# Four graph layers on 32 pairs of graphs: the pairs under way start 14 steps apart instead of 7

## The chip, the core and the metric

The kernel runs on one core of a Trainium2 chip. The metric is the time of one execution on the device in microseconds (us). The engines of the core work side by side, each through its own queue in order: TensorE (PE in the profile; its weight loads are PEld), VectorE (DVE), ScalarE (ACT), GpSimd (POOL), and SyncE (SP), which issues the transfers. TensorE writes into PSUM, which VectorE and ScalarE read; the rest lies in SBUF.

## What is computed

64 graphs of 256 nodes with 256 features go through four layers. Each normalizes x, cuts it off at 0, applies a graph layer and adds the result to x. All of it is float32.

```python
# layer 0: 8 heads of 32, softmax over the neighbours (adj > 0), output projection
h = relu(layernorm(x)); x = x + mha(h, adj, Wq, Wk, Wv) @ Wo + bo
# layer 1: e = leaky(f1[i] + f2[j]), masked by adj, softmax over axis 1, elu of the sum
h = relu(layernorm(x)); x = x + elu(softmax(where(adj > 0, e, -9e15), axis=1) @ (h @ W))
# layer 2: three rounds of a gated unit on the sums over the neighbours
h = relu(layernorm(x))
for i in range(3): h = gru(A.T @ (h @ weight[i]), h)
x = x + h
# layer 3: 4 heads of 64, additive attention, softmax over the neighbours (adj == 1)
h = relu(layernorm(x)); x = x + gat(h, adj, W, b, a)
```

## The kernel before, in words

Two graphs, a **pair**, go through all four layers together, so there are 32 pairs. A pair's x and adj are loaded as one tile each (io pool, 4 buffers), and x stays in SBUF until layer 3 has stored it. Each layer is a generator: a `yield` ends a **step**, and a pair takes 44 steps.

- Layer 0, steps 1 to 13: mask mb0 and norm (L268, L226 to L234); transposes psn and hT (L241, L243); q, k, v (L278, L250); then for each of 4 row blocks a `scores` step (pss L300, s = min(scaled scores, mask) L307, row maxima mx L260, eight exponentials with sums L262) and an `attend` step (16 transposes pst L327, copies to pT by VectorE L334 and ScalarE L332, psc L341 with pT as weights and 32-wide moving operands, ctxs L348), the scores one block ahead; then transposes psct and the projection pso (L250).
- Layer 1, steps 14 to 18: mask (L379 to L391), norm, one softmax over 256 columns (L409 to L421), product psh (L427), elu and sum (L435 to L438).
- Layer 2, steps 19 to 33: mask am and norm, then three times four steps: psgm and its copy m (L250, L451); psa and its copy aT (L457, L465); the gates r, hn and n (L475, L491 to L507); gate z and the new state hg (L491, L494, L512 to L514). The products of the gates are 512 wide. At the end hg is transposed back (psx L520) and added to x (L521).
- Layer 3, steps 34 to 44: mask mb3 (L526, L527), norm, f and sd (psf L536, L537; pssd L548, copies by ScalarE L549), then 4 blocks of `scores` (L554 to L561, L260, four exponentials L262) and `attend` (8 transposes pst L572, copy eT by ScalarE L574, pso L580, o L588, sum on GpSimd L594); the last one issues the store.

The main loop at the end sets the order. Up to three pairs are under way, and in each turn of the loop each of them takes one step, the oldest first. A new pair starts when the youngest has taken at least `LEAD` steps and fewer than three are under way. With 44 steps and a lead of 7, the first three start at turns 0, 7 and 14; the fourth starts when the first has ended, and so the pattern of 0, 7 and 14 repeats each 44 turns, a **round** of three pairs. Three pairs of a round are called its first, second and third below. The last round has two pairs.

The framework gives each instruction to its engine's queue nearly in this order, but may put a later instruction that it takes to be ready ahead of an earlier one; on the chip each queue is then in order. Buffers come from pools, by tag: `w4` (token tiles, 17 buffers), `w8` (scores and their transposes, 4), `hT` (4), `f3` (1, L530), `mask` (2), and PSUM tiles of two banks (4). A tile waits until a buffer of its tag is released.

```python
            ps = bank2(f"psc_{p}_{t}")
            for i in range(H0):
                h = 4 * (i % 2) + i // 2
                for c in range(2):
                    mm(ps[:, 0, h * D0 : (h + 1) * D0], pT[:, i, c, :],
                       v[:, 2 * g + c, h * D0 : (h + 1) * D0], start=c == 0, stop=c == 1)
```

Of the kernel before, what the change touches and what calls it, by code (L numbers as in the profile page):

```python
# [9 lines left out]
FP = mybir.dt.float32  # L10
# [5 lines left out]
P = 128  # L16
# [8 lines left out]
def tile_adj_preln_d4(  # L25
# [18 lines left out]
    a3: bass.AP,  # L44
    out: bass.AP,
):
    """Four pre-norm graph layers on B graphs of N nodes.

    Two graphs go through all layers together. "Token" tiles are [node in chunk, t, feature] with
    t = 2 * graph + chunk; "T" tiles are [feature in chunk, feature chunk, 2 * N nodes].  # L50
    """
    nc = tc.nc
    B, N, D = x.shape
    NL = ggw.shape[0]
    H0, H3 = 8, a3.shape[0]
    D0, C3 = D // H0, D // H3
    assert N == 2 * P and D == 2 * P and B % 2 == 0 and H0 == 8 and H3 == 4
    T = 4  # token tiles in a pair
    N2 = 2 * N
    SCALE = 1.0 / math.sqrt(D0)  # L60

# [2 lines left out]
    psum = ctx.enter_context(tc.tile_pool(name="psum", bufs=4, space=bass.MemoryType.PSUM))  # L64

    def bank2(name):
        """Two PSUM banks."""
        return psum.tile([P, 2, 512], FP, tag="ps", name=name)

    def flat(ap):  # L70
# [10 lines left out]

    loaded = {0: loads(0)}

# [1 line left out]
    ident = const.tile([P, P], FP, name="ident")  # L85
    make_identity(nc, ident)
    mhalf = const.tile([P, T], FP, name="mhalf")
# [39 lines left out]
    with tc.tile_pool(name="prep", bufs=1) as prep:  # L127

        def transposed(dst, src, rows):
            """dst[:, k, :] = rows k of the transpose of src [P, rows / P, D]."""  # L130
            n = rows // P
            for k in range(2):
                for o in range(0, n, 4):
                    m = min(4, n - o)
                    ps = bank2(f"tw_{k}_{o}")
                    for i in range(m):
                        nc.tensor.transpose(
                            ps[:, 0, i * P : (i + 1) * P],
                            src[:, o + i, k * P : (k + 1) * P],
                            ident,  # L140
                        )
                    nc.vector.tensor_copy(dst[:, k, o * P : (o + m) * P], ps[:, 0, 0 : m * P])

        for w, wT, nm in ((w_ih, wihT, "wih_sb"), (w_hh, whhT, "whh_sb")):
            t = prep.tile([P, 6, D], FP, tag="wg", bufs=2, name=nm)
            nc.sync.dma_start(t, w.rearrange("(k p) d -> p k d", p=P))
            transposed(wT, t, 3 * D)
        # r and z are taken as (1 + tanh(v / 2)) / 2.
        nc.vector.tensor_add(brz, bih_sb[:, 0:4], bhh_sb[:, 0:4])
        nc.vector.tensor_scalar_mul(brz, brz, 0.5)  # L150

        # Layer 1: f1 = h (W a_1), f2 = h (W a_2).
        w1T = prep.tile([P, 2, D], FP, name="w1T")
        transposed(w1T, w1a, D)
        a1_sb = prep.tile([P, 2, 2], FP, name="a1_sb")
        nc.sync.dma_start(a1_sb.rearrange("p w k -> p (w k)"), a1.rearrange("(c p) e -> p (c e)", p=P))
        for f in range(2):
            ps = bank2(f"wa_{f}")
            for k in range(2):
                mm(ps[:, 0, 0:2], w1T[:, k, f * P : (f + 1) * P], a1_sb[:, :, k], start=k == 0, stop=k == 1)  # L160
            wa = prep.tile([P, 2], FP, tag="wa", bufs=2, name=f"wa_sb_{f}")
            nc.vector.tensor_copy(wa, ps[:, 0, 0:2])
            nc.vector.tensor_copy(wa1_bc[:, f, :], wa[:, 0:1].to_broadcast([P, P]))
            nc.vector.tensor_copy(w1a[:, f, D : D + 1], wa[:, 1:2])

        # Layer 3: s_src = h (W^T a_src) + b a_src, s_dst likewise; a's rows on a block diagonal.
        w3_sb = prep.tile([P, 2, D], FP, name="w3_sb")
        nc.sync.dma_start(w3_sb, w3.rearrange("(k p) o -> p k o", p=P))
        transposed(w3a, w3_sb, D)
        blk = prep.tile([P, 2, 2, H3], FP, name="blk")  # L170
        nc.vector.memset(blk, 0.0)
        for h in range(H3):
            r0 = (h * C3) % P
            for w in range(2):
                nc.sync.dma_start(
                    blk[r0 : r0 + C3, h * C3 // P, w, h : h + 1],
                    a3[h : h + 1, w * C3 : (w + 1) * C3].rearrange("o c -> c o"),
                )
        for f in range(2):
            ps = bank2(f"w3s_{f}")  # L180
            for k in range(2):
                mm(
                    ps[:, 0, 0 : 2 * H3],
                    w3_sb[:, k, f * P : (f + 1) * P],
                    blk[:, k].rearrange("p w h -> p (w h)"),
                    start=k == 0,
                    stop=k == 1,
                )
            nc.vector.tensor_copy(w3a[:, f, D : D + H3], ps[:, 0, 0:H3])
            ws = prep.tile([P, H3], FP, tag="ws", bufs=2, name=f"ws_{f}")  # L190
            nc.vector.tensor_copy(ws, ps[:, 0, H3 : 2 * H3])
            nc.vector.tensor_copy(wdst_bc[:, f], ws.unsqueeze(2).to_broadcast([P, H3, P]))
        b3_sb = prep.tile([P, 2], FP, name="b3_sb")
        nc.sync.dma_start(b3_sb, b3.rearrange("(k p) -> p k", p=P))
        b3_w = prep.tile([P, 2, P], FP, name="b3_w")
        nc.vector.tensor_copy(b3_w, b3_sb.unsqueeze(2).to_broadcast([P, 2, P]))
        blk_s = prep.tile([P, 2, H3], FP, name="blk_s")
        nc.vector.tensor_add(blk_s, blk[:, :, 0, :], blk[:, :, 1, :])
        ps = bank2("b3s")
        for k in range(2):  # L200
            mm(ps[:, 0, 0:H3], b3_w[:, k, :], blk_s[:, k, :], start=k == 0, stop=k == 1)
        nc.vector.tensor_copy(b3a_bc[:, D : D + H3], ps[:, 0, 0:H3])

# [1 line left out]
    work = ctx.enter_context(tc.tile_pool(name="work", bufs=2))  # L205
    small = ctx.enter_context(tc.tile_pool(name="small", bufs=4))

    def w4(name):
        """A token tile."""
        return work.tile([P, T, D], FP, tag="w4", bufs=17, name=name)  # L210

    def w4T(name):
        return w4(name).rearrange("p (a b) d -> p a (b d)", a=2)
# [2 lines left out]
        return work.tile([P, H0, N], FP, tag="w8", bufs=4, name=name)  # L216

    def mask(name):
        return work.tile([P, T, N], FP, tag="mask", bufs=2, name=name)

    def norm_relu_T(xt, nm):
        """T tile of relu(layernorm(xt))."""
        st = small.tile([P, T, 6], FP, tag="st", name=f"st_{nm}")
        mv = small.tile([P, T, 2], FP, tag="mv", name=f"mv_{nm}")
        for t in range(T):
            nc.vector.bn_stats(st[:, t, :], xt[:, t, :])  # L226
        for t in range(T):
            nc.vector.bn_aggr(mv[:, t, :], st[:, t, :])  # L228
        rs = small.tile([P, T], FP, tag="rs", name=f"rs_{nm}")
        nc.gpsimd.tensor_scalar_add(rs, mv[:, :, 1], EPS)  # L230
        nc.gpsimd.tensor_tensor(rs, rs, mhalf, ALU.pow)
        xn = w4(f"xn_{nm}")
        for t in range(T):
            nc.vector.tensor_scalar(  # L234
                xn[:, t, :], xt[:, t, :], mv[:, t, 0:1], rs[:, t : t + 1], ALU.subtract, ALU.mult
            )
        yield
        ps = bank2(f"psn_{nm}")
        for k in range(2):
            for t in range(T):  # L240
                nc.tensor.transpose(ps[:, k, t * P : (t + 1) * P], xn[:, t, k * P : (k + 1) * P], ident)  # L241
        hT = work.tile([P, 2, N2], FP, tag="hT", bufs=4, name=f"hT_{nm}")
        nc.scalar.activation(hT, ps, AF.Relu)  # L243
        return hT

    def token_mm(rhs, hT, ps4):
        """ps4[t] = h rhs, node chunk by node chunk."""
        for t in range(T):
            for k in range(2):
                mm(ps4[t], hT[:, k, t * P : (t + 1) * P], rhs[:, k, :], start=k == 0, stop=k == 1)  # L250
# [4 lines left out]
        return v, [v[:, t, :] for t in range(T)]  # L255

    def exp_rows(e, n, zs, nm):
        """e[:, i] = exp(e[:, i] - max) in place for i < n, and their sums in zs."""
        mx = small.tile([P, n], FP, tag=f"mx{n}", name=f"mx_{nm}")
        nc.vector.tensor_reduce(mx, e, AX.X, ALU.max, negate=True)  # L260
        for i in range(n):
            nc.scalar.activation(  # L262
                e[:, i, :], e[:, i, :], AF.Exp, bias=mx[:, i : i + 1], accum_out=zs[:, i : i + 1]
            )

    def layer0(xt, at, p):
# [7 lines left out]
        for w, nm in ((wq_sb, "q"), (wk_sb, "k")):  # L274
# [4 lines left out]
            t = w4T(f"{nm}T_{p}")  # L279
# [5 lines left out]
        v = w4(f"v_{p}")  # L285
# [2 lines left out]

        ctxs = w4(f"ctxs_{p}")

        # Head h = 4 * cc + hh lies on partitions 32 * hh of feature chunk cc; rows are (hh, cc).
        def scores(t):
            g = t // 2
            s = w8(f"s_{p}_{t}")
# [146 lines left out]
    def layer2(xt, at, p):  # L441
# [4 lines left out]
        for l in range(NL):  # L446
# [60 lines left out]
                nc.scalar.activation(hn[:, o, :], hn[:, o, :], AF.Tanh, bias=bih_sb[:, 4 + o : 5 + o])  # L507
            yield
            z = sigmoid(2, "z")
            # (1 - z) n + z h = n + z (h - n)  # L510
            hnew = work.tile([P, 2, N2], FP, tag="hT", bufs=4, name=f"hg_{nm}")
            nc.gpsimd.tensor_sub(hnew, hT, hn)  # L512
            nc.vector.tensor_mul(hnew, hnew, z)
# [98 lines left out]
        for layer in (layer0, layer1, layer2, layer3):  # L612
            yield from layer(xt, at, p)

    # Pairs start LEAD steps apart, so that one's matrix products fill another's softmax and norms.
    LEAD, UNDER_WAY = 7, 3
    active, p = [], 0
    while active or p < B // 2:
        if p < B // 2 and (not active or (len(active) < UNDER_WAY and active[-1][1] >= LEAD)):
# [39 lines left out]
```

## Time and profile before

| | |
|---|---|
| median of three timed runs | 6370.5 us (6350.5 to 6374.0) |
| the profiled execution, first to last instruction | 6365.3 us |
| mean granted TensorE clock in it | 0.890 of full speed |
| TensorE matmul busy | 5787.0 us (91%), 24500 records |
| TensorE weight load busy | 3967.9 us (62%) |
| VectorE busy | 3090.6 us (49%) |
| ScalarE busy | 2004.0 us (31%) |
| GpSimd busy | 777.0 us (12%) |
| transfers | 58.4 MB, 9 GB/s over the span |

The page gives the span of the profiled execution, 6365.3 us; the timed runs have no profile, and their median is 5.2 us above it. A float32 product stands in the trace as two records, a transpose as one. A group of instructions is named by its line, its engine and its tiles (out<-in); buffer and pair numbers are left out, so that psn is the transposed norm of any layer, and `pso` is the projection of layer 0 at L250 and the output of layer 3 at L580. In a list of waits each line gives who waited for whom, the total, the number of times and the longest one. A granted clock of 1.00 is full speed.

### The profile page before, as it was taken

The numbers are of one execution on the slowest core, as the hardware profiler recorded it, in microseconds if no ns is written. First come the engines' busy times: TensorE is split into PE (matmuls) and PEld (weight loads), VectorE is DVE, ScalarE is ACT, GpSimd is POOL, SyncE is SP. The second block draws the span as 40 slices with busy tenths as digits, with TensorE's granted clock in tenths as the row PEclk, the third lists the DMA queues.
The fourth block names the chain that finished last, engine by engine and source line by source line (L and its number), as shares of the span: only waits on it lengthen the run. The fifth ranks groups of instructions, "written<-read, shape, count | busy, mean of one in ns | idle before, by whom it ended". The sixth has DMA issues, their size and how long they took to land.

```text
span 6365.3 us, 60565 instructions
## 1 busy us (share of the span) xinstructions
PE 5787.0 (91%) x24500; PEld 3967.9 (62%) x24500; DVE 3090.6 (49%) x4479; ACT 2004.0 (31%) x4737; POOL 777.0 (12%) x582
## 2 busy tenths in 40 slices
PE   7998899889989988998899889889988998999887
PEld 6655765666566556655765665576557656665755
DVE  4435534554454445445544553554455345534534
ACT  2323322332233233223322332242233223322422
POOL 1011101100110111011001101110110011001011
PEclk7899799889978997898899889978987998899798
DMA  1000000000000000000000000000000000000000
GB/s 53 1 4 19 9 1 7 17 7 1 14 17 1 4 14 14 1 4 20 7 1 14 17 1 4 14 14 1 4 20 7 1 7 17 7 1 10 7 0 7
DMA packets 58279, 58.40 MB, mean 9 GB/s; under 512 B 4752, under 2 KB 58000, under 8 KB 58000
## 3 DMA queue, kind: packets, MB, share of 16 engines
q1 hardware_dynamic: 58000, 54.54, 2.6%
q8 instruction: 192, 3.15, 0.2%
q14 instruction: 87, 0.71, 0.0%
HBM read 37.76 MB, written 16.78 MB: 9 GB/s over the span
## 4 chain that ended last, share of the span: by engine, by line
PE 78%; DVE 13%; ACT 8%; issue 1%; DMA 0%; POOL 0%; SPq 0%; ACTq 0%; POOLq 0%; DVEq 0%
PE psr L475 10%; PE psz L475 10%; PE psc L341 9%; PE psin L475 5%; PE pshn L475 5%; PE psa L457 5%; PE pso L580 5%; PE psgm L250 4%; PE pssd L548 3%; PE pss L300 3%; DVE mx L260 3%; PE psq L278 2%; ACT s L262 2%; PE pso L250 2%; PE psf L536 2%; ACT eT L574 2%
## 5 line engine op out<-in xcount | busy, mean ns | idle before, releaser
L341 PE MATMUL psc<-v,pT 128*128 128x32 f32 x4096 | 621.6, 316 | 146.1 <-DVE pT L334 143.6
L341 PEld LDWEIGHTS psc<-v,pT 128*128 128x128 f32 x4096 | 612.1, 237 | 198.7 <-DVE pT L334 92.6
L262 ACT ACTIVATE s<-s,mx 128x256 f32<-128x256 f32 x1024 | 506.8, 499 | 304.5 <-DVE mx L260 166.0
L262 ACT ACTIVATE e<-e,mx 128x256 f32<-128x256 f32 x640 | 318.0, 500 | 630.6 <-DVE mx L260 630.5
L580 PE MATMUL pso<-f,eT 128*128 128x64 f32 x2048 | 323.1, 324 | 193.6 <-ACT eT L574 193.5
L580 PEld LDWEIGHTS pso<-f,eT 128*128 128x128 f32 x2048 | 302.8, 234 | 228.9 <-ACT eT L574 228.9
L307 DVE SCALAR_TENSOR_TENSOR s<-pss,mb 128x1024 f32<-128x1024 f32 x256 | 306.8, 1219 | 176.4 <-PE pss L300 176.4
L457 PE MATMUL psa<-am,m 128*128 128x256 f32 x1536 | 369.5, 396 | 2.3 <-ACT m L451 2.2
L475 PE MATMUL psz<-aT,wihT 128*128 128x512 f32 x768 | 363.6, 596 | 0.0
L475 PE MATMUL psr<-aT,wihT 128*128 128x512 f32 x768 | 363.3, 593 | 0.0
L475 PE MATMUL psin<-aT,wihT 128*128 128x512 f32 x768 | 345.2, 592 | 0.0
L457 PEld LDWEIGHTS psa<-am,m 128*128 128x128 f32 x1536 | 298.8, 199 | 47.6 <-ACT m L451 7.2
L327 PE MATMUL pst<-ident,s 128*128 128x128 f32 x2048 | 297.7, 307 | 18.7 <-DVE pT L334 14.5
L494 DVE TENSOR_SCALAR z<-z 128x1024 f32<-128x1024 f32 x96 | 66.6, 693 | 493.9 <-ACT z L491 493.9
L327 PEld LDWEIGHTS pst<-ident,s 128*128 128x128 f32 x2048 | 278.2, 163 | 32.8 <-DVE pT L334 17.1
L260 DVE TENSOR_REDUCE mx<-s 128x8 f32<-128x2048 f32 x128 | 292.0, 2281 | 1.2
L243 ACT ACTIVATE hT<-psn 128x1024 f32<-128x1024 f32 x128 | 130.9, 1022 | 488.8 <-PE psn L241 488.7
L348 DVE TENSOR_TENSOR ctxs<-psc,rz 128x256 f32<-128x256 f32 x128 | 54.4, 425 | 459.7 <-PE psc L341 459.7
L230 POOL TENSOR_SCALAR rs<-mv 128x4 f32<-128x4 f32 x128 | 33.7, 263 | 1973.1 <-DVE mv L228 1730.7
L475 PEld LDWEIGHTS psz<-aT,wihT 128*128 128x128 f32 x768 | 148.6, 194 | 191.0 <-issue 191.0
L250 PE MATMUL psgm<-gg_sb,hg 128*128 128x256 f32 x1024 | 254.4, 405 | 14.4 <-DVE hg L514 14.4
L594 POOL TENSOR_TENSOR x<-o,x 128x256 f32<-128x256 f32 x128 | 118.9, 929 | 1177.9 <-DVE o L588 1164.4
(140 smaller groups left out, 10040.8 us busy)
## 6 DMA issues: line engine op xcount, KB each, us to landing
x<-in_x_dram SPq DMA_DIRECT2D x32, 512.0 KB, 3.4
adj<-in_adj_dram SPq DMA_DIRECT2D x32, 512.0 KB, 3.3
out_dram<-x SPq DMA_DIRECT2D x32, 512.0 KB, 2.9
gg_sb<-in_L_gnn_weight_dram SPq DMA_DIRECT2D x3, 256.0 KB, 6.3
wih_sb<-in_L_gnn_w_ih_dram SPq DMA_DIRECT2D x1, 768.0 KB, 6.4
whh_sb<-in_L_gnn_w_hh_dram SPq DMA_DIRECT2D x1, 768.0 KB, 7.2
wq_sb<-in_L_gnn_Wq_dram SPq DMA_DIRECT2D x1, 256.0 KB, 5.4
wk_sb<-in_L_gnn_Wk_dram SPq DMA_DIRECT2D x1, 256.0 KB, 5.6
```

Of the source, the lines that this page charges most:

```text
L243: nc.scalar.activation(hT, ps, AF.Relu)
L250: mm(ps4[t], hT[:, k, t * P : (t + 1) * P], rhs[:, k, :], start=k == 0, stop=k == 1)
L260: nc.vector.tensor_reduce(mx, e, AX.X, ALU.max, negate=True)
L262: nc.scalar.activation(e[:, i, :], e[:, i, :], AF.Exp, bias=mx[:, i : i + 1], accum_out=zs[:, i : i + 1])
L300: mm(ps[:, j, cc * N : (cc + 1) * N], qT[r : r + D0, cc, t * P : (t + 1) * P], kT[r : r + D0, cc, g * N : (g + 1) * N], start=True, stop=True,
L307: nc.vector.scalar_tensor_tensor(s[:, 4 * half : 4 * half + 4, :], ps.rearrange("p a (b d) -> p (a b) d", d=N), SCALE, mb0[:, t : t + 1, : ...
L327: nc.tensor.transpose(psr[:, 2 * i + c, :], s[:, 4 * half + i, c * P : (c + 1) * P], ident)
L341: mm(ps[:, 0, h * D0 : (h + 1) * D0], pT[:, i, c, :], v[:, 2 * g + c, h * D0 : (h + 1) * D0], start=c == 0, stop=c == 1,)
L457: mm(psa[:, o, g * N : (g + 1) * N], m[:, 2 * g + c, o * P : (o + 1) * P], am[:, 2 * g + c, :], start=c == 0, stop=c == 1,)
L475: mm(ps[:, o, :], w[:, k, c0 : c0 + P], src[:, k, :], start=n == 0, stop=n == 2 * len(terms) - 1,)
L548: mm(ps[:, j, :], wdst_bc[:, k, 2 * half + j, :], hT[:, k, :], start=k == 0, stop=k == 1)
L580: mm(pso[:, 0, h * C3 : (h + 1) * C3], eT[:, 2 * h + c, :], f[:, 2 * g + c, h * C3 : (h + 1) * C3], start=c == 0, stop=c == 1,)
```

## The change

The lead becomes 14 steps, about a third of the 44. The three pairs of a round then start at turns 0, 14 and 28, and this pattern repeats. `mask` gets a third buffer, and `w4` 16 buffers instead of 17; a buffer of either takes 4 KB of each partition. Nothing else of the program changes but comments.

```diff
     def w4(name):
-        return work.tile([P, T, D], FP, tag="w4", bufs=17, name=name)
+        return work.tile([P, T, D], FP, tag="w4", bufs=16, name=name)
...
     def mask(name):
-        return work.tile([P, T, N], FP, tag="mask", bufs=2, name=name)
+        return work.tile([P, T, N], FP, tag="mask", bufs=3, name=name)
...
-    LEAD, UNDER_WAY = 7, 3
+    LEAD, UNDER_WAY = 14, 3
     active, p = [], 0
     while active or p < B // 2:
         if p < B // 2 and (not active or (len(active) < UNDER_WAY and active[-1][1] >= LEAD)):
```

## The prediction

> **What bounds the kernel now.** I read first the page's busy shares and slices, then stretches of one round of three pairs, then TensorE's waits, then the order of time around them.
>
> ```profile
> PE 5787.0 (91%) x24500; PEld 3967.9 (62%) x24500; DVE 3090.6 (49%) x4479; ACT 2004.0 (31%) x4737; POOL 777.0 (12%) x582
> PE   7998899889989988998899889889988998999887
> PEclk7899799889978997898899889978987998899798
> ```
> TensorE is the busiest by far, but its digits and its clock dip together, about ten times: once in each round of three pairs. A round is 587.5 us: TensorE starts psq of pair 3 at 594.3 us and of pair 30 at 5882.0, and (5882.0 - 594.3) / 9 = 587.5. One round, cut by how many pairs are in layer 2 (none, one, two, one):
>
> ```profile
> 2356.00:2573.00 217.00, 186.16 (x997) 146.82 (x995) 121.50 (x163) 84.20 (x241) 25.13 (x20) 0.79 0.04 13
> 2573.00:2677.00 104.00, 99.81 (x422) 68.67 (x422) 44.32 (x71) 28.27 (x63) 8.92 (x8) 0.91 0.00 1
> 2677.00:2851.00 174.00, 169.98 (x554) 99.59 (x553) 69.40 (x97) 45.78 (x76) 17.79 (x11) 0.99 0.01 3
> 2851.00:2948.00 97.00, 83.73 (x325) 52.95 (x323) 53.81 (x88) 29.23 (x64) 20.63 (x15) 0.94 0.05 17
> ```
> The columns are length, busy PE, PEld, DVE, ACT, POOL, then the granted clock. With no pair in layer 2 TensorE idles 31 of 217 us and its clock is 0.79; with two it idles 4 of 174 at 0.99. The clock is worth as much as the idle time:
>
> ```profile
> 2372.23 2.00 PE L580 MATMUL pso<-f,eT 128*128 128x64 f32 x16 [1.16 <-ACT eT L574]
> ...
> 2407.52 3.68 PE L580 MATMUL pso<-f,eT 128*128 128x64 f32 x16 [1.10 <-ACT eT L574]
> ```
> The same 16 matmuls take 2.00 us and 3.68 us: the trace's clock record knows only full and half speed. From start to start at full speed a 512-wide matmul record takes 0.43 us, a 256-wide one 0.217, psc 0.113, pso of layer 3 0.115, a transpose 0.111, pss 0.09. Times the counts of the groups: 4608 x 0.43 (L475) + 5632 x 0.217 + 1152 x 0.43 (L278, L396, L548) + 4096 x 0.113 + 2048 x 0.115 + 4864 x 0.111 + 2048 x 0.09 = 5120 us, 160 a pair, 480 a round. The span is then 5120 work + 578 idle (6365.3 - 5787.0) + 667 lost mostly to half clock. In rounds 2 to 10 (5289 us, 4846 busy): **480 work + 49 idle + 58 half clock = 587**. The change can touch only the last two. Who ends the idle time:
>
> ```profile
> PE pso L580 <- ACT eT L574: 193.5, 127, 5.9
> PE psc L341 <- DVE pT L334: 143.6, 97, 4.7
> PE psx L520 <- DVE hg L514: 88.9, 22, 6.8
> PE psn L241 <- DVE xn L234: 44.6, 12, 5.2
> ```
> The columns are total us, times, longest. The first two are built into the steps: transposes, a copy, and the matmuls that read the copy stand in a row on TensorE.
>
> **The change, part by part.** No instruction is added or removed. (1) The mask buffer more and the w4 buffer less: the trace shows no wait for either. A pair holds one mask at a time, so three pairs need three. For w4 I bound the loss by the f3 buffer's waits (L530 has one; VectorE waits for it at L537 21 times, 208 us in all, and TensorE's pso then waits 5.9 us instead of 1.2): from nothing to 32 x 5 = 160 us. I take nothing, since the order below holds no trace of a shortage. (2) f3's conflict ends: with 14 steps between, layer 3 of one pair is over before the next writes f3. TensorE gets back 10 x 4.5 us = 4.5 a round. (3) The head and tail: 44 steps a pair, so 491 steps become 498. (4) The order. The order of instructions of the two built programs (without times) shows what TensorE finds between a producer's last matmul and the consumer that waits for it. I call the sum of full-speed matmul time between them the cover, and match it with the waits that the same link had before.
>
> - pT to psc: always 0.9 us of cover in both. Before 145.9 us for 128 groups; 0.9 a group without the long ones. Ten a round: **9 us**.
> - eT to pso: no cover 127 times before, 118 after, 1.2 us each when nothing else is late. Eleven a round: **13 us**.
> - hg to psx or psgm: before, cover 0 gave waits of 6.8 us, 3.5 gave 1.3, over 5 none. After there is one psgm without cover (about 5), one psx with 0.9 (6), three with 2.7 to 4.2 (1.3 each): **15 us**, against 10.
> - Out of layer 1. psh's output goes through L435 to L438, the norm and xn before psn can start, and this chain is 9 us of VectorE, ScalarE and GpSimd work with nothing between. Before, the cover was 9 us or more in every round, and only one pair in three waited:
>
> ```profile
> 3128.30 1.23 DVE L435 TENSOR_SCALAR ex<-psh 128x1024 f32<-128x1024 f32 x1 [2.23 <-PE psh L427]
> ...
> 3141.51 2.27 DVE L260 TENSOR_REDUCE mx<-s 128x8 f32<-128x2048 f32 x1
> ...
> 3145.53 1.38 DVE L234 TENSOR_SCALAR xn<-x,mv,rs 128x256 f32<-128x256 f32 x4 [0.35 <-POOL rs L231]
> ```
> Another pair's L307 and mx stand between on VectorE's queue. After, the cover is 13.3, 3.8 and 1.8 us for a round's first, second and third pair, because the next pair now enters layer 0 just there. I walk the queues by hand: 1.15 us for a 1024-wide VectorE operation in a row, 2.2 for mx, 1.7 for stats and aggregates, 1.5 for GpSimd's rs. *Second pair*, psh's end at 0: L435 from 1.0, then L307, L437, L307, L438 to 6.8, mx to 9.0, L521 to 10.2, norm to 11.9, rs to 13.4, psn at 14.0; TensorE has work until 3.8: **10.2 us**. Next on VectorE are L307, mx and the other pair's norm, so pT ends at 21.1 where pst was done at 17: **4.2 us** at psc. *Third pair*: psh waits 2.1 for wh, psn 6.3: **8.4 us**.
> - *First pair*: psn is covered, but the psc that follows is not. The next pair's pT stands behind layer 3's e, which waits for the sd copies that ScalarE makes after eight exponentials: mx 8.3, exponentials 13.9, sd 15.9; then five operations of 1.15, mx 2.2 and mx 1.1 to 25.2, pT to 26.4. pst is done at 16: **10.3 us**.
>
> Idle in a round: 9 + 13 + 15 + 10.2 + 4.2 + 8.4 + 10.3 = **70 us**, against 49.
>
> Half clock. By the clock record, a whole psc group beside a layer 2 (the third pair before) cost 2.3 to 3.3 us, without layer 2 up to 7.2; groups that the order cuts in two by a wide matmul cost nothing; layer 3's pso 0.9 on the mean; psx's 6.8 us wait about 2.5. After: 7 whole psc x 2.9 = 20, two psc that run into a pso at 5 = 10, 8 other pso x 0.9 = 7, three long waits x 2.5 = 7.5, and the two psc behind a 10 us wait 4 more each = 8: **52 us**, against 58. Layer 2 beside every softmax ends each half-clock spell sooner, but no longer gives TensorE a stretch without any.
>
> A round: 480 + 70 + 52 = **602 us**, nine 5418. *Head*: 352 us of work up to psq of pair 3 (before 453). Setup 28; the first 68 us of work are pair 0 alone, with waits such as the trace's first ones and norms without cover, 30 idle and 20 half clock: 118; the rest 284 x 602/480 = 356: 502. *Tail*, from psq of pair 30: 448 us of work. 317 x 602/480 = 398; 107 of the last layer 2 beside one layer 3, with 24 of waits and 8 of clock: 139; then the last layer 3 alone, about 68 from its last psz (before 79 from 6286.5 to the end, with a rest of pair 30 in it): 605. Sum 5418 + 502 + 605 = 6525, against the profiled 6365.3. The median of the runs is 5.2 above that span; so **6530 us**, 2.5% more.
>
> [...] With TensorE as in the stretch of two layers 2 (170 of 174 us busy) a round would be near 500 and the kernel near 5500; the walks above speak against it. [...]
>
> **Rivals.** *A, evenly fed TensorE wins* (faster): the walks fail, say because a late TensorE lets VectorE clear its queue. Idle 40 (49 less f3's 4.5 and psn's 4.2), half clock 9 x 2.9 + 8 + 3 = 37: a round 557, head 475, tail 575, in all 6065. For it: the clock of 0.91 to 0.99 beside layer 2. Against it: before, one layer 2 at a time (2573 to 2677, 2851 to 2948) had 18 idle us in 201, no better than the mean. It decides if the four long waits come out under some 4 us each. *B, half of it*: the long waits at half length, idle 60, half clock 50: a round 590, head 495, tail 597, in all about 6405. *C, worse*: w4 waits or more half clock, 625 a round: about 6755. *D, it doesn't do what it says*: excluded by the order, which has one pair in layer 2 at nearly every step.
>
> **How the numbers follow.** Forecast (6450 to 6650) 0.55, B (6320 to 6450) 0.25, A 0.13, C 0.07. The range leaves out most of A and C: 6290 to 6680. Faster by over 0.5% (about what a measurement of this kernel can tell from no change) takes A and a little of B: 0.16; within 0.5% 0.14; slower 0.70.
>
> **What would show it.** Slices without the ten dips in PE and PEclk; L537's wait for pso gone; TensorE's wait of psn for xn at some 15 us a round (44.6 in all before, over 140 after), of psc for pT over 200 in all; mean clock about 0.90 still. I am wrong if psn's and psc's waits stay where they were, or if the mean clock rises above 0.93.

## The result and the profile after

The changed kernel takes 6593.9 us (median of four runs, 6588.1 to 6597.0) against 6366.7 (6350.5 to 6374.0) for the kernel before in the same runs: a ratio of 1.0368, 95% interval 1.0348 to 1.0387. The forecast was 6530, and slower. The profiled execution spans 6589.3 us at a granted clock of 0.881 (before 6365.3 at 0.890).

The page of the kernel after, its first part and two rows of its slices:

```profile
PE 5828.3 (88%) x24500; PEld 3965.9 (60%) x24500; DVE 3105.2 (47%) x4479; ACT 2009.4 (30%) x4737; POOL 790.0 (12%) x582
...
PE   7898889889888988898898898888998899898887
...
PEclk7898899888889888898889898988888899889887
```
The ten dips of before are gone, as foretold, but so are many of the nines (12 of 40 slices of PE, against 19). TensorE is busy 41 us longer (5828.3 against 5787.0) with the same instructions, and idle for 761 us against 578.

One round, cut where TensorE starts psq of the second, third and next first pair; columns as in the prediction (length, busy PE, PEld, DVE, ACT, POOL, granted clock, DMA):

```profile
2330.40:2523.20 192.80, 175.72 (x747) 118.02 (x747) 85.37 (x125) 58.64 (x137) 24.92 (x18) 0.89 0.03 9
2523.20:2719.10 195.90, 174.45 (x741) 119.83 (x740) 91.27 (x127) 61.84 (x147) 19.68 (x15) 0.88 0.02 6
2719.10:2941.40 222.30, 194.99 (x808) 131.70 (x807) 113.45 (x168) 67.73 (x160) 29.34 (x22) 0.88 0.03 10
```
Each third idles 17 to 27 us at 0.88 or 0.89. Before, stretches from 0.79 to 0.99 stood side by side. The load is even, and evenly poor. TensorE's waits in the kernel after:

```profile
PE psn L241 <- DVE xn L234: 167.7, 38, 8.1
PE psc L341 <- DVE pT L334: 161.8, 127, 6.9
PE pso L580 <- ACT eT L574: 150.6, 118, 3.1
PE psgm L250 <- DVE hg L514: 109.2, 44, 4.7
PE psx L520 <- DVE hg L514: 59.9, 21, 5.3
```
psn's wait for xn went from 44.6 to 167.7 us and psgm's for hg from 14.4 to 109.2; pso's fell from 193.5 to 150.6 and psx's from 88.9 to 59.9. VectorE's wait for pso at L537, 208 us before, is no longer in its list.

Where the time is lost is best seen in **rounds**. I take the stretch from psq of pair 3 to psq of pair 30, nine rounds; idle is its length less busy PE; the rest is what is left over the 480 us of full-speed work. Half speed is the time per round in which the trace's clock record stands at half. TensorE is idle in some of it: 9.8 us a round before, 20.8 after. By the durations of the records I estimate that some 5 or 6 us of the rest, in both kernels, are not half speed.

| kernel | round, us | idle | rest | half speed |
|---|---|---|---|---|
| before | 587.5 | 49.2 | 58.3 | 121.7 |
| after | 608.8 | 65.1 | 63.7 | 139.2 |

So of 21.3 us more in a round 15.9 are idle time and 5.4 are clock; nine rounds make 191 of the 224 us by which the span grew. The rest is in the head, 504.3 us, and the tail, 606.2 (before 594.3 and 483.3).

Which products paid for the clock is seen in the groups of matmuls. First the kernel before (busy, mean ns of one | idle time just before them):

```profile
L457 PE MATMUL psa<-am,m 128*128 128x256 f32 x1536 | 369.5, 396 | 2.3 <-ACT m L451 2.2
...
L300 PE MATMUL pss<-kT,qT 32*128 32x256 f32 x2048 | 259.7, 565 | 0.4
...
L250 PE MATMUL psgm<-gg_sb,hg 128*128 128x256 f32 x1024 | 254.4, 405 | 14.4 <-DVE hg L514 14.4
```
and the same three after:

```profile
L457 PE MATMUL psa<-am,m 128*128 128x256 f32 x1536 | 454.7, 462 | 3.6 <-ACT m L451 3.6
...
L250 PE MATMUL psgm<-gg_sb,hg 128*128 128x256 f32 x1024 | 368.8, 538 | 109.2 <-DVE hg L514 109.2
...
L300 PE MATMUL pss<-kT,qT 32*128 32x256 f32 x2048 | 165.7, 407 | 23.8 <-DVE s L307 23.8
```
psc and pso of layer 3 cost the same in both (619 against 622, 321 against 323). But before, pss often stood in half-speed spells behind psc: 1254 of its 2048 records began in such a spell, and in groups of 16 that ran wholly at half speed one took 131 ns on the mean, against a median of 72 in those at full speed. After, 56 begin there. psa and psgm stand there now (189 records before, 1138 after), and such a record takes 427 ns instead of 216. They pay 200 us more (85.2 and 114.4 by the lines), pss 94 less. All other groups together cost some 64 less (pst 50 and psq 29 of it, with some others up), which leaves the 41 us.

### The profile page after: what moved, and what is told of

Read it like the earlier page. It is cut to its first block, busy times and chain, and to the rows that moved or that the text cites. A ratio compares the mean times of both kernels' runs of the same rounds, so it can differ in the third digit from the quotient of the medians.

```text
span 6589.3 us, 60281 instructions
## 1 busy us (share of the span) xinstructions
PE 5828.3 (88%) x24500; PEld 3965.9 (60%) x24500; DVE 3105.2 (47%) x4479; ACT 2009.4 (30%) x4737; POOL 790.0 (12%) x582
## 4 chain that ended last, share of the span: by engine, by line
PE 72%; DVE 18%; ACT 7%; issue 1%; POOL 1%; DMA 0%; SPq 0%; DVEq 0%; ACTq 0%; POOLq 0%
PE psr L475 9%; PE psc L341 9%; PE psz L475 8%; PE psgm L250 8%; PE psa L457 7%; PE pshn L475 4%; PE pso L580 4%; PE psin L475 3%; DVE mx L260 3%; PE pssd L548 2%; DVE s L307 2%; DVE pT L334 2%; PE psq L278 2%; PE psn L241 2%; ACT s L262 2%; PE pso L250 2%
## 5 line engine op out<-in xcount | busy, mean ns | idle before, releaser
L341 PE MATMUL psc<-v,pT 128*128 128x32 f32 x4096 | 619.0, 315 | 174.6 <-DVE pT L334 161.8
L262 ACT ACTIVATE e<-e,mx 128x256 f32<-128x256 f32 x640 | 316.9, 496 | 556.1 <-DVE mx L260 556.1
L250 PE MATMUL psgm<-gg_sb,hg 128*128 128x256 f32 x1024 | 368.8, 538 | 109.2 <-DVE hg L514 109.2
L457 PE MATMUL psa<-am,m 128*128 128x256 f32 x1536 | 454.7, 462 | 3.6 <-ACT m L451 3.6
L580 PE MATMUL pso<-f,eT 128*128 128x64 f32 x2048 | 321.4, 323 | 150.6 <-ACT eT L574 150.6
L457 PEld LDWEIGHTS psa<-am,m 128*128 128x128 f32 x1536 | 360.3, 240 | 81.1 <-issue 10.4
L250 PEld LDWEIGHTS psgm<-gg_sb,hg 128*128 128x128 f32 x1024 | 283.9, 285 | 183.8 <-DVE hg L514 80.0
L241 PE MATMUL psn<-ident,xn 128*128 128x128 f32 x1024 | 200.2, 344 | 169.6 <-DVE xn L234 167.7
L494 DVE TENSOR_SCALAR r<-r 128x1024 f32<-128x1024 f32 x96 | 66.6, 694 | 545.9 <-ACT r L491 545.9
L507 ACT ACTIVATE hn<-hn,bih_sb 128x512 f32<-128x512 f32 x192 | 128.1, 714 | 634.9 <-DVE hn L505 634.9
L241 PEld LDWEIGHTS psn<-ident,xn 128*128 128x128 f32 x1024 | 159.4, 177 | 219.1 <-DVE xn L234 104.0
L334 DVE COPY pT<-pst 128x1024 f32<-128x1024 f32 x128 | 156.1, 1219 | 278.9 <-PE pst L327 278.9
L451 ACT COPY m<-psgm 128x1024 f32<-128x1024 f32 x96 | 97.3, 1013 | 607.0 <-PE psgm L250 607.0
```

Source lines behind the costliest of these rows:

```text
L262: nc.scalar.activation(e[:, i, :], e[:, i, :], AF.Exp, bias=mx[:, i : i + 1], accum_out=zs[:, i : i + 1])
L334: nc.vector.tensor_copy(dst, flat(ps))
L341: mm(ps[:, 0, h * D0 : (h + 1) * D0], pT[:, i, c, :], v[:, 2 * g + c, h * D0 : (h + 1) * D0], start=c == 0, stop=c == 1,)
L457: mm(psa[:, o, g * N : (g + 1) * N], m[:, 2 * g + c, o * P : (o + 1) * P], am[:, 2 * g + c, :], start=c == 0, stop=c == 1,)
L580: mm(pso[:, 0, h * C3 : (h + 1) * C3], eT[:, 2 * h + c, :], f[:, 2 * g + c, h * C3 : (h + 1) * C3], start=c == 0, stop=c == 1,)
```

## The experiments

All ratios are to the kernel before on the same chip, with their 95% intervals; it took 6362 to 6368 us in each case. The changed kernel was not timed again, and its 6593.9 us stand in the comparisons with it. First the rounds of all twelve, as in the table above:

| kernel | median us | ratio | round | idle | rest | half speed |
|---|---|---|---|---|---|---|
| 1: lead 11 | 6625.6 | 1.0422 (1.0386 to 1.0457) | 614.3 | 64.7 | 69.6 | 159.7 |
| 2: lead 16 | 7279.8 | 1.1451 (1.1413 to 1.1489) | 675.8 | 101.3 | 94.5 | 225.3 |
| 3: lead 14, later psn | 6474.4 | 1.0184 (1.0150 to 1.0218) | 597.7 | 64.3 | 53.4 | 123.7 |
| 4: lead 14, split attends | 6409.4 | 1.0073 (1.0039 to 1.0107) | 590.9 | 65.5 | 45.4 | 123.6 |
| 5: lead 7, new buffers | 6399.3 | 1.0060 (1.0037 to 1.0084) | 591.6 | 48.1 | 63.5 | 133.9 |
| 6: lead 14, wide | 6175.1 | 0.9708 (0.9693 to 0.9723) | 570.0 | 66.8 | 23.2 | 51.2 |
| 7: lead 7, wide | 6016.6 | 0.9459 (0.9444 to 0.9474) | 556.0 | 56.2 | 19.8 | 33.8 |
| 8: lead 14, 3 and 4 together | 6302.7 | 0.9909 (0.9893 to 0.9925) | 580.3 | 58.3 | 42.0 | 116.1 |
| 9: lead 7, wide, split layer 0 | 6115.9 | 0.9605 (0.9570 to 0.9640) | 566.6 | 62.0 | 24.6 | 54.2 |
| 10: lead 14, wide, 3 and 4 | 5969.4 | 0.9375 (0.9346 to 0.9403) | 549.5 | 50.8 | 18.7 | 51.2 |
| 11: lead 14, only psc wide | 6289.0 | 0.9876 (0.9846 to 0.9907) | 580.3 | 66.5 | 33.8 | 75.1 |
| 12: lead 7, wide, new buffers | 6019.7 | 0.9452 (0.9423 to 0.9481) | 556.1 | 55.7 | 20.4 | 39.1 |

My theory at first was the prediction's: the waits follow from how much of TensorE's work the order puts between a producer and its consumer (the cover), and the clock follows the waits loosely. The rival was that spreading the pairs costs in itself.

### 1 and 2: other leads

```diff
-    LEAD, UNDER_WAY = 14, 3
+    LEAD, UNDER_WAY = 11, 3      # 1; 16 in 2
```


> The changed kernel with a lead of 11 steps instead of 14 (pairs at turns 0, 11, 22 of 44), all else as changed. Theory 1 (waits at the joints): what a lead costs is set by which link finds no cover on TensorE. In the built order with 11, psn behind psh and psx/psgm behind hg are covered nearly as with 7 (links that come out short add up to about 27 us of wait a round of three pairs, against 23 with 7 and 44 with 14). Idle near 50 a round, half clock near 60, so 590 a round and 6370 to 6430 in all. Rival (spreading itself costs, since half-clock spells fall on layer 2's wide products): 11 lies between 7 and 14 and so does its time, near 6500.

> The changed kernel with a lead of 16 (pairs at turns 0, 16, 32; the gaps are 16, 16 and 12, as even as 14, 14 and 16). Theory 1: the short links add up to about 59 us a round (psh behind psw 26, psx and psgm behind hg 24) against 44 with 14, so about 15 us a round more than with 14: 6690 to 6800 in all. Rival (spreading itself costs): as even as 14, so as slow, 6590 within 30.

Both theories missed both kernels. Lead 11 was to be better than 14 and, with 6625.6 us, is not; lead 16 takes 7279.8. In lead 11 idle is as after (64.7), but it stands elsewhere. One psc waits 10.6 us for pT, once a round. VectorE in that wait:

```profile
2590.72 1.22 DVE L307 SCALAR_TENSOR_TENSOR s<-pss,mb 128x1024 f32<-128x1024 f32 x1
2591.86 1.22 DVE L438 SCALAR_TENSOR_TENSOR x<-psh,ex 128x1024 f32<-128x1024 f32 x1
2592.99 2.28 DVE L260 TENSOR_REDUCE mx<-s 128x8 f32<-128x2048 f32 x1
2595.18 1.22 DVE L560 SCALAR_TENSOR_TENSOR e<-e 128x1024 f32<-128x1024 f32 x1
...
2600.17 1.20 DVE L334 COPY pT<-pst 128x1024 f32<-128x1024 f32 x1
```
The copy stands behind operations of three pairs (layer 0's s and mx, layer 1's elu and the norm after it, layer 3's e). Cover on TensorE says nothing of this queue, and counting it did not rank the leads. With lead 16 a pair of 44 steps ends four turns before the next may start, so a round has 48 turns with three gaps of 16 (the expectation took the third as 12), and in 12 of the 48 only two pairs are under way. It is thus no pure test of the distance. Idle is 101.3 us a round, with a psh wait in each third of it:

```profile
2772.17 3.74 PE L404 MATMUL psw<-w1a,hT 128*128 128x257 f32 x16
2786.79 6.68 PE L427 MATMUL psh<-wh,e 128*128 128x256 f32 x16 [10.88 <-DVE wh L421]
```
And half speed costs most there: 2000 of the 2048 pso records of layer 3 begin at half speed (630 before). So the distance by itself does not rank the leads. In the chain of lead 11 it is the operations of the other pairs that fall between; that this decides it in general is argued, not shown.

### 3 and 4: two links given cover, lead 14

```diff
     # 3: after layer 2's norm, xn to psn
-        yield
+        for _ in range(1 + late): yield          # late = 1 in layer 2, else 0
     # 4: layers 0 and 3, attend becomes a generator
             (transposes and copies)
+            yield
             (psc, or pso of layer 3)
```


> The changed kernel (lead 14) with one step more between layer 2's xn and its transposes psn, so that TensorE has a whole step of other pairs' work there. Theory 1: psn's wait for xn (167.7 us) goes almost wholly, hg's wait grows by about 5 us a round in the built order, so some 8 to 12 us a round less: 6480 to 6530. Rival (VectorE's queue is late anyway, and TensorE only meets the same delay at the next wait, psc for pT or psgm for hg): 6570 to 6600, with psc's wait for pT up by what psn's loses.

> The changed kernel (lead 14) with one step more in each attend of layers 0 and 3, between the transposes with their copies and the products psc and pso that read the copies. Theory 1: pso's wait for eT (150.6 us) and most of psc's wait for pT (174.5) go, about 25 us a round; other links in the built order stay as short as they are; half clock falls little, since the 32-wide products themselves bring it about: 6330 to 6430. Rival (the clock follows the waits): half clock falls with the waits, by 20 a round more, 6200 or less. Second rival (VectorE's queue decides): the waits reappear elsewhere, 6550 to 6600.

The times, 6474.4 us (6 below my theory's range) and 6409.4 (within it), are about what my theory asked for, but the reason is not. TensorE's waits in kernel 3,

```profile
PE psx L520 <- DVE hg L514: 203.5, 32, 7.8
...
PE psn L241 <- DVE xn L234: 21.2, 16, 6.3
```
and in kernel 4:

```profile
PE psn L241 <- DVE xn L234: 259.3, 55, 8.3
PE psgm L250 <- DVE hg L514: 214.4, 54, 5.7
...
PE pso L580 <- ACT eT L574: 5.6, 4, 2.2
```
Each repair removed the wait it aimed at (psn from 168 to 21; psc and pso from 162 and 151 to 2 and 6) and other links took it over: idle stays at 64.3 and 65.5 of 65.1 us. The whole gain in a round is in the rest, 63.7 to 53.4 and 45.4. So the clock is a lever of its own, and what moves it had to be found. One thing more changes: the added steps make a pair 45 and 52 steps long at the same lead, so the starts are 14, 14 and 17 or 24 turns apart, and other meetings between pairs shift too. Neither kernel tests a repair with all else equal.

### 5: the buffers alone

```diff
-        return work.tile([P, T, D], FP, tag="w4", bufs=17, name=name)
+        return work.tile([P, T, D], FP, tag="w4", bufs=16, name=name)
...
-        return work.tile([P, T, N], FP, tag="mask", bufs=2, name=name)
+        return work.tile([P, T, N], FP, tag="mask", bufs=3, name=name)
```


> The new buffer counts (three masks, 16 token tiles) with the lead of before, 7 steps. If the loss is all in the order of the three pairs' steps, this is the kernel before over again: 6345 to 6385 us, ratio 0.997 to 1.003. If the buffers themselves take part (a mask written earlier stands in front of other work on VectorE and GpSimd): 6420 us or more.

6399.3 us, 36 more than before: outside the range of "nothing", and below the other. In the built program, taking only the w4 buffer away leaves the order of instructions exactly as it was, with 22 more waits on ScalarE; the third mask, which lets masks be written earlier, moves instructions on TensorE, VectorE, ScalarE and GpSimd. So the mask is the likely cause, but neither was run alone. Idle is as before (48.1, against 49.2), and the rest is 5.2 us a round more. It is again the clock.

### 6, 7 and 11: narrow products made wide

Where do the spells of half speed begin? In the traces before and after all but one spell of each last a whole multiple of 3.41 us, so I looked at the 3.4 us ahead of each. Of 167 spells before and 202 after, 113 each begin behind 3.4 us of which psc and pso took over 30%; and in 67 and 53 cases TensorE was busy for over 70% of that time, in 22 and 24 for over 99%, where no wait in that time explains them. One of them, in the kernel after, first its matmuls and then two stretches (columns as in the round above, the granted clock before the last two):

```profile
2413.36 1.91 PE L327 MATMUL pst<-ident,s 128*128 128x128 f32 x16
2415.71 3.90 PE L341 MATMUL psc<-v,pT 128*128 128x32 f32 x32 [0.44 <-DVE pT L334]
2419.42 5.26 PE L457 MATMUL psa<-am,m 128*128 128x256 f32 x16
...
2415.80:2419.10 3.30, 3.30 (x31) 3.30 (x31) 2.21 (x2) 0.57 (x1) 0.00 (x0) 1.00 0.00 0
2419.20:2422.50 3.30, 3.30 (x10) 2.72 (x10) 1.55 (x2) 1.27 (x5) 0.00 (x0) 0.50 0.00 0
```
psc kept TensorE busy without a stop, and the clock fell all the same. psc moves 32 columns, pso 64. A 128-wide transpose takes 111 ns at full speed, psc 113: by these two, width up to 128 should be free. So psc and pso move 128 columns of v and f; the columns that belong to other heads land in PSUM where nothing reads them.

```diff
-                        ps[:, 0, h * D0 : (h + 1) * D0],
+                        ps[:, i % 2, 96 * (i // 2) : 96 * (i // 2) + P],
                         pT[:, i, c, :],
-                        v[:, 2 * g + c, h * D0 : (h + 1) * D0],
+                        v[:, 2 * g + c, (i % 2) * P : (i % 2 + 1) * P],
...
-                        pso[:, 0, h * C3 : (h + 1) * C3],
+                        pso[:, 0, P * h - C3 * (h % 2) : P * h - C3 * (h % 2) + P],
                         eT[:, 2 * h + c, :],
-                        f[:, 2 * g + c, h * C3 : (h + 1) * C3],
+                        f[:, 2 * g + c, (h // 2) * P : (h // 2 + 1) * P],
```
(L348 and L588 read the useful columns at a stride of 128. Kernel 11 has only the first half.)

> The kernel after, with layer 0's products psc moved 128 columns wide in place of 32 and layer 3's products pso 128 in place of 64 (the further columns are not read; the results are the same). Theory: the half-speed spells begin in stretches filled with narrow products, however busy TensorE is; then most of the 63.7 us of half clock in a round goes (20 to 30 stay), at 111 to 115 ns for a product at full speed as before, since a 128-wide transpose takes 111: 6110 to 6220 us, granted clock 0.94 or more. Rival: the spells follow from TensorE's waits, which stay: 6570 to 6640 us, clock 0.88. Second rival: wider products cost by their width: 6700 us or more.

> The same widening on the kernel before (lead 7). Theory of the narrow products: of the 58.3 us of half clock in a round 20 to 30 stay: 5960 to 6060 us, clock 0.94 or more. Rival, spells follow from waits: 6350 to 6410 us, clock 0.90. If the theory holds, the ratio between the widened kernels at leads 14 and 7 shows the idle part of the loss alone: 16 us of a round, about 1.027.

> The kernel after with only layer 0's products psc widened from 32 to 128 columns; layer 3's products pso keep 64. Widening both gave 6175 us, 419 less than the kernel after. If the narrower a product the more half-speed spells it begins: psc gives two thirds or more of it, 6175 to 6320 us. Rival, pso begins as many spells as psc: 6370 to 6430 us.

6175.1, 6016.6 and 6289.0 us: all three as the theory of the narrow products has it. Kernel 6, its clock and two groups:

```profile
PEclk8999999999999999999999999999999999999998
...
L341 PE MATMUL psc<-v,pT 128*128 128x128 f32 x4096 | 554.9, 299 | 183.0 <-DVE pT L334 163.1
...
L580 PE MATMUL pso<-f,eT 128*128 128x128 f32 x2048 | 277.5, 292 | 173.1 <-ACT eT L574 173.1
```
Four times as many columns take less time (psc 619.0 to 554.9 us) because more of them run at full speed (582 of 4096 begin at half speed, 1248 in the kernel after), where a 128-wide record takes 112 to 116 ns. TensorE's idle time did not shrink (66.8 us a round, against 65.1), and half speed fell from 139 to 51 us a round; so most of the half speed did not follow from the waits alone. The spells that stay begin otherwise: behind 3.4 us in which TensorE was busy for over 70% stand 1 of 90 in kernel 6, 1 of 141 in kernel 11 and none of 74 in kernel 7, and the mean busy share in kernel 6 is 29% (55% in the kernel after). So they go with idle time; this is read from where they stand, and no run tests it. Widening psc alone brings 305 of the 419 us. And kernel 6 against 7 shows what spreading costs with most of the half speed gone: 6175.1 / 6016.6 = 1.026, of 14.0 us a round 10.6 idle and 3.4 clock. The widened kernels do not wait quite as their parents do: by the idle column 1.7 us a round more at lead 14, and 7 us at lead 7.

Few spells follow a long stop: in the 6.8 us ahead of a spell TensorE stood still for over 3.4 us at a stretch (the shortest spell lasts 3.41) in 20 of 167 cases before, 27 of 202 after and 14 of 90 in kernel 6, where the idle time is mostly made of shorter waits. And with nearly the same idle time (65.1, 66.5 and 66.8 us a round in the kernel after and in kernels 11 and 6) the width of the products sets half speed to 139, 75 or 51 us a round.

### 12: the buffers alone, wide

> The widened kernel at lead 7 with the third mask and 16 token tiles. Without the widening these buffers alone cost 36 us, with TensorE's idle time per round unchanged (48.1 against 49.2). If that loss was half clock alone, it goes with the half clock: 6005 to 6035 us. If it lies in the order of VectorE and GpSimd: 6045 us or more.

6019.7 us against 6016.6 for kernel 7. The 36 us of the new buffers go with the narrow products (3 are left), so they were half clock.

### 8, 9 and 10: what is left

Kernel 8 is 3 and 4 together; kernel 10 is 8 with wide products; kernel 9 is 7 with layer 0's attend split.

> Lead 14 with both repairs: layers 0 and 3 yield between an attend's transposes and its products, and layer 2 yields twice after its norm. If each repair takes away the waits of its own links and leaves the others (psn took 259 us in the split kernel, and the later yield took 147 of 168 in the unsplit one but gave 144 to psx): 6260 to 6340 us. If what one link is spared only moves to the next one: 6390 to 6440 us.

> Lead 7 and the buffers of before, both products widened, and layer 0 alone yields between an attend's transposes and its products. The widened kernel at lead 7 takes 6016.6 us and waits 216 us for pT. If the yield takes those waits away and nothing takes their place: 5820 to 5890 us. Rival, which the two earlier repairs speak for (in both TensorE's idle time per round stayed at 64 to 66 us, against 65.1): the idle time moves to other links: 5950 to 6030 us.

> Lead 14 with both repairs (split attends in layers 0 and 3, the later step after layer 2's norm) and both products widened. If widening takes away only what the half clock still costs in the repaired kernel (42 us of a round, down to about 20): 6050 to 6090 us. Rival, the two gains add in full (6303 less the 419 us that widening gave the unrepaired kernel): 5880 us.

Kernel 8, 6302.7 us, is in the range of its theory and has 58.3 us idle: with both links mended part of the idle time does go. Kernel 9 missed both ranges, at 6115.9 us, 99 more than without the split (its lines behind the split have numbers one higher):

```profile
PE pso L581 <- ACT eT L575: 237.9, 118, 8.0
PE psh L428 <- DVE wh L422: 101.0, 22, 7.8
...
PE psc L342 <- DVE pT L334: 26.9, 14, 3.4
```
psc's wait is mostly gone (216 to 27), psh has 86 us more, and idle rose from 56.2 to 62.0 us a round, the rest from 19.8 to 24.6. The pairs now take 48 steps with the same lead, so the meetings on VectorE are new; that they are worse ones is my reading of the waits, no chain was followed. Kernel 10, in the stretch of nine rounds:

```profile
500.10:5446.00 4945.90, 4488.95 (x20629) 3054.44 (x20628) 2610.25 (x3753) 1680.21 (x3996) 653.88 (x486) 0.95 0.03 9
```
4945.9 less 4489.0 is 457 us idle, 50.8 a round. At 5969.4 us it is the fastest of all and between my two forecasts: the repairs are worth 206 us with wide products (6175.1 to 5969.4) and 291 without, where they moved the clock too. So a lead of 14 need not be slow: with its links covered and wide products its round is 549.5 us, against 556.0 of kernel 7. But a pair has 53 steps there, and the starts are 14, 14 and 25 turns apart, no longer even; and lead 7 with both repairs wasn't tried, since layer 3's split needs more buffers there than the kernel has. So which lead is better is not shown.

## Why the prediction was right, and where it was not

- **The sum.** A round of 602 us was foretold and 608.8 measured; head 502 and 504.3; tail 605 and 606.2. The span came out 64 us longer than the sum, 61 of it nine rounds of 6.8. The direction and most of the size came out of the waits. That the round is within 7 us is partly luck: idle time was foretold 5 us too high and half clock 12 too low.
- **Ordinary psc and pso links**: 9 and 13 us a round foretold; 7.6 and 14.0 measured (mean waits by pair and block in rounds 2 to 10).
- **hg links**: 15 foretold, 15.7 measured, with some luck in the parts: the psgm of the third pair's second gate round waits 3.5 us where I had it in the class of 1.3, psx 5.3 instead of 6, and the other psgm 4.7, 1.6 and up to 0.5.
- **psn of the second pair, 10.2 us foretold, 6.4 measured.** VectorE in this link, after:

```profile
2740.99 1.22 DVE L435 TENSOR_SCALAR ex<-psh 128x1024 f32<-128x1024 f32 x1
2742.12 1.22 DVE L307 SCALAR_TENSOR_TENSOR s<-pss,mb 128x1024 f32<-128x1024 f32 x1
...
2745.61 1.22 DVE L438 SCALAR_TENSOR_TENSOR x<-psh,ex 128x1024 f32<-128x1024 f32 x1
2746.74 2.28 DVE L260 TENSOR_REDUCE mx<-s 128x8 f32<-128x2048 f32 x1
...
2753.20 1.38 DVE L234 TENSOR_SCALAR xn<-x,mv,rs 128x256 f32<-128x256 f32 x4 [0.36 <-POOL rs L231]
```
The order is the walk's own. psh ends at 2739.9; L435 was to start 1.0 us later and psn 14.0, and they start at 1.1 and 13.8. But TensorE, which was to run dry at 3.8, has work until 7.0: two pss behind psh wait 1.1 and 1.2 us for s. The long wait was cut into three, 9.1 us in all in this round.
- **psc of the second pair's first block, 10.3 us foretold, 6.8 measured.** VectorE needs 10.2 us from layer 3's e to pT's end (walk: 10.5), but pst ends 3.5 us after e's start instead of 0.1; its second half waits 1.0 us for s itself. The walk had TensorE on time and so gave too long a wait.
- **psc of the third pair** 4.2 foretold, 2.2 measured; **psh and psn of the third pair** 2.1 and 6.3, measured 1.6 and 6.3.
- **Idle in all**: 70 foretold, 65.1 measured. In the two long links above, TensorE's earlier stops shortened the wait.
- **Half clock, the term that failed: 52 us foretold, 63.7 measured; a gain of 6 became a loss of 5.** The step was "Layer 2 beside every softmax ends each half-clock spell sooner, but no longer gives TensorE a stretch without any". The spells did get a little shorter (121.7 us in 15.3 spells a round before, 8.0 each; 139.2 in 18.7 after, 7.4 each) but more numerous, and I counted them by psc, pso and the long waits, at the prices of before. psc and pso cost the same as before; the bill came from the products behind them, psgm and psa of layer 2 (200 us more) in place of pss (94 less). The term had the narrow products in it as a price per group, without asking why the clock falls there; kernels 6 and 11 show that their width makes most of the half speed (139.2 us a round fell to 51.2 and 75.1), with the idle time nearly unchanged (65.1, 66.8 and 66.5).
- **Buffers at nothing.** The two buffers together, taken as harmless, cost 36 us at lead 7 through the clock, most likely by the third mask; what they cost at lead 14 can't be told apart, as that lead needs the mask.
- **f3's conflict ends** as foretold: L537's wait for pso is gone, and pso's longest wait fell from 5.9 to 3.1 us.
- **The signs**: psn's wait is 167.7 us, as foretold (over 140). psc's wait for pT was to be over 200 in all and is 161.8, 174.5 with ScalarE's copies; it was not what marked the change. The mean clock, 0.881, is below the 0.90 of the forecast.
- **Rival A** (6065) asked for idle 40 and half clock 37 in a round, and fell on both. Its time is beaten by kernel 10, but by wide products: the 50.8 us idle there are still above the rival's 40.
- **What stays open**: the exact rule by which the clock falls. Width is shown as a cause; how width and idle time combine is not. Nor is it shown why one distance between pairs lines VectorE's chains up worse than another; for leads 11 and 14 single chains were followed, for 16 only the wait was seen.

## What to carry to other kernels

When pipelined streams share engines in order, the distance between them is no dial of its own: it decides which chains meet in each engine's queue, and each wait must be walked there: here leads of 7, 11, 14 and 16 gave rounds of 587.5, 614.3, 608.8 and 675.8 us, and the work on the busiest engine did not rank them. Removing one wait in such an order can move it (in kernels 3 and 4 idle stayed at 64.3 and 65.5 of 65.1 us), so judge a repair by the idle time of a whole period and not by the wait it aimed at. And before ordering for the clock, look at what makes it fall: here products of 32 and 64 moving columns, which cost no less than 128 (112 ns a record at full speed), let a busy TensorE fall to half speed (22 of 167 spells before begin behind 3.4 us in which it was busy for over 99%), and widening them (5.4% at lead 7) was worth more than any reordering without it (0.9%).

## What the runs showed of the hardware that I had not expected

- A float32 product record takes the same time with 32, 64 and 128 moving columns: the median from start to start within a group is 112 ns at full speed and 213 at half, for psc and pso of the kernel before and of kernel 6 alike.
- TensorE falls to half speed while busy with 32- and 64-wide products (67 of 167 spells before begin behind 3.4 us in which it was busy for over 70%, 22 behind over 99%): widening psc alone took half speed from 139.2 to 75.1 us a round, pso as well to 51.2, with idle time at 65 to 67 us throughout.
- What a half-speed spell costs depends on what stands in it: some 60 ns a record for pss (32 rows, 256 columns; 72 become 131), some 211 for psa or psgm (216 to 427).
